# Graph attention on one core: rulers ahead of the gathers, and a new order for the last steps

## The chip, the cores and the metric

The kernel runs on one core of a Trainium2 chip. The metric is the time of one execution on the device in microseconds (us), the median of several runs; lower is better. A core has five engines with a queue of instructions each: TensorE (PE, matrix products and transposes; its weight loads are listed as PEld), VectorE (DVE), ScalarE (ACT), GpSimd (POOL) and SyncE (SP). Transfers are started by an instruction in one of the queues and then run by themselves on 16 DMA engines; in the listings SPq and ACTq are the starts of transfers in the queues of SP and ACT. SBUF is the on-chip memory (128 partitions), PSUM the small memory into which PE writes.

## What is computed

One layer of a graph network: N = 12,500 nodes with 128 features, E = 212,500 edges sorted by their destination, 8 heads of 16 features.

```python
h = relu(layernorm(x))                       # nodes
q = h @ Wq.T + bq;  v = h @ Wv.T + bv        # nodes
k = edge_attr @ Wk.T + bk                    # edges
qs, qd = q[src], q[dst]                      # edges
in_m, out_m, diag_m = sum(qs * k), sum(qd * k), sum(qs * qd)   # over each head's 16
score = (softmax_by_dst(in_m * SCALE) + softmax_by_dst(out_m * SCALE)
         + softmax_by_dst(diag_m * SCALE)) * edge_weight ** lam
agg = segment_sum(score * v[dst], dst)
out = x + leaky_relu(agg @ Wo.T + bo, 0.1)
```

As v[dst] is the same for all edges of a segment, the kernel sums only scores (24 numerators and 24 denominators a node) and multiplies by v once for each node.

## The kernel before

All of it is in the function `ordered_path`. The helper `pin` (L596) ties an instruction to the pinned one before it on the same engine, so each engine executes in the written order; the order of the work is therefore written out by hand. Instructions that aren't pinned are placed where they are written, but only their data bind them.

**Preparation** (L734 to L1014). The nodes come in in groups, DVE takes their statistics (L886 to L909), ACT normalizes (L921), PE transposes (L929, copied at L931) and multiplies with Wq (L937), DVE adds the bias (L940), and the rows of q go to a table in HBM, `q_table`. The first 40 gathers on POOL (L691) fetch raw rows of x instead, since the table isn't ready; from the twelfth on they are paced by DVE's groups of nodes. The function `show` (L750 to L758) makes `shows`, a small matrix of "rulers": POOL counts up two tiles by iota (`of_f` L752, `of_row` L755), and DVE compares the first (L757) and casts the second (L758). `raw_indices` (L763 to L768) makes the indices of the raw gathers.

**The main loop.** The edges are cut into 416 blocks of 512; the last one, with 20 edges, is treated apart. The other 415 are spread over S = 5 streams of G = 83 blocks, so that a turn t takes block t of each stream, and a step g = 5t + s handles one block. In each step:

- POOL gathers q[src] for step g + 20, four indirect transfers of 128 rows (`gather`, L691);
- PE transposes the edge features two steps ahead (`turn`, L1154; ACT copies at L1156), multiplies them with Wk one step ahead (`project`, L1161 and L1163), and spreads q[dst] from a window of the table with one-hot matrices (`spread_q`, L1171; ACT copies `qd` at L1174 and makes the one-hots at L1148 and L1149);
- DVE forms the three products (L1184 and L1185) and, once for two steps, sums them over heads' features into the logits `lT` (L1190).

For each turn, two turns later and spread over its steps: PE transposes the logits (`turn_logits`, `l_ps`, L1211), DVE scans forward for the running maximum of each segment (`scan_on`, L1244 and L1249) and back (`scan_back`, L1262), for which ACT first spreads a mask into PSUM (`spread_far`, `far_ps`, L1255); PE turns the maxima (`turn_max`, `m_ps`, L1332), `powers` subtracts them (DVE, L1340) and exponentiates (ACT, L1341), `weigh_powers` multiplies with the weights (L1352), and `to_rows` sums edges into nodes by a matrix product with the selection `sel` (L1380, copied by ACT at L1385). `select` (SP, L1358) loads where the segments end and `show_ends` makes `sel` from it: per turn two products with the rulers into `d_ps` (L1366), two absolute values (L1369) and one rectifier (L1370) on ACT. `put_rows` (SP, L1396) stores the sums of a turn, one transfer a stream, at row addresses that SP has read into its registers in `fetch` (the register load is at L626). `l_ps`, `far_ps`, `m_ps`, `d_ps`, `w_ps` and the nodes' `node_ps` share one ring of three PSUM buffers (`small`, L1202).

**Finishing nodes.** As turns are stored, pairs of node groups are finished between the steps by the class `Nodes`: `load_x`, `load_sums` (SP at L1061, for nodes at the border of two streams also ACT at L1063), `normalize` (L1070), `turn` (L1080, copied at L1083), `project_v` (product with Wv, L1086 and L1088), `scores` (L1030 to L1036), `weigh` (L1096), `project_o` (product with Wo, L1107), `add_x` (L1112 and L1113) and `store` (L1119, L1121). What is at the border of streams can only be finished at the end: `rest`, five groups with 18 tiles of 128 nodes, begun in the last steps by `begin_rest`; the products with Wv that wait for their scores are made by `hold` into banks of PSUM.

**The tail** (L1555 to L1609) is what follows the last step: the logits and scans of the last turns G−2, G−1 and G (G is the block of 20 edges), their powers and sums, the storing of these sums, then `load_sums` of the five groups, the last ordinary pair, and the groups' scores, weighings and outputs. The scores of all 18 tiles are made by one pass of `scores_of`.

Of the kernel before, what the change touches and what calls it, by code (L numbers as in the profile page):

```python
# [472 lines left out]
def ordered_path(ctx: ExitStack, tc: tile.TileContext, flag, x, src, dst, edge_attr, edge_weight,  # L473
# [144 lines left out]
    def fetch(t):  # L618

        if t >= T:  # L620
            return
        far = load.tile([R, BE + 1], BF, name="far", bufs=4)
        lo = t * BE
        of = bass.AP(far_d.tensor, far_d.offset + lo, [[G * BE, S], [0, H3], [1, BE + 1]])
        pin(nc.sync.dma_start(far, of))
        _, base_v[t] = nc.values_load_multi_w_load_instructions(  # L626
            bases[0:1, t:t + (S - 1) * G + 1:G], engines=[mybir.EngineType.SP], min_val=0, max_val=N - 1,
            skip_runtime_bounds_check_because="the indices of nodes are below N")
        st[t] = dict(far=far)
# [104 lines left out]
    with tc.tile_pool(name="prep", bufs=1) as prep, \  # L734
# [14 lines left out]

        def show():  # L750
            of = prep.tile([K4, JN, S, W], F32, name="of_f", tag="of", bufs=2)
            nc.gpsimd.iota(of, pattern=[[1, JN], [JN, S], [0, W]], base=1, channel_multiplier=-1,  # L752
                           allow_small_or_imprecise_dtypes=True)
            row = prep.tile([1, JN, S, W], F32, name="of_row", tag="of", bufs=2)
            nc.gpsimd.iota(row, pattern=[[0, JN], [0, S], [1, W]], base=1, channel_multiplier=0,  # L755
                           allow_small_or_imprecise_dtypes=True)
            nc.vector.tensor_scalar(shows, of, 0.0, -1.0, op0=ALU.is_equal, op1=ALU.mult)  # L757
            nc.vector.tensor_copy(shows[0:1], row)  # L758
# [279 lines left out]
    class Nodes:  # L1038
# [52 lines left out]
        def project_v(self, to):  # L1091
            self.held = to
# [39 lines left out]
    with tc.tile_pool(name="work", bufs=2) as work, \  # L1132
# [228 lines left out]
        def show_ends(t):  # L1361

            sel = st[t]["sel"] = work.tile([P, JN, S, W], F32, name="sel", bufs=3)
# [24 lines left out]
        def put_rows(t, of=range(S)):  # L1388
            for i, (lo, own) in enumerate(trios):
                for k in own:  # L1390
# [5 lines left out]
                    pin(nc.sync.dma_start(  # L1396
# [84 lines left out]
        products = str(mybir.EngineType.PE)  # L1481
        fetch(1)
# [10 lines left out]
        for g in range(end):  # L1493
# [39 lines left out]
            later(put_rows, t - 2 if s == 4 else t - 3, [(s + 1) % S])  # L1533
            if t == G - 1:
                if 0 < s < 4:
                    select(G - 3 + s)
                elif s == 4:
                    for i in (G - 2, G - 1, G):
                        show_ends(i)
# [6 lines left out]
            begin_rest(g - (end - BEGIN))  # L1546
            if g < S:
# [7 lines left out]
        leaving, last_pair = pairs[G - 3], pairs[G - 1]  # L1555
# [3 lines left out]
        last_pair.scores()  # L1559
        last_pair.turn(small([P, JN, P], "node_ps"))  # L1560
        scan_on(G - 1)
        hold(rest[0], True)
        more_banks()
        last_pair.project_v(banks.pop(0))
        scan_back(G - 2)
        turn_max(G - 2)
        scan_on(G)
        scan_back(G - 1)
        turn_max(G - 1)
        scan_back(G)  # L1570
        turn_max(G)
        for t in (G - 2, G - 1, G):
            powers(t)
        for t in (G - 2, G - 1, G):
            weigh_powers(t)
        last_pair.weigh(last_pair.held)
        for t in (G - 2, G - 1, G):
            to_rows(t)
            put_rows(t)
        for r, of in enumerate(rest):  # L1580
            of.load_sums(ends_ab[:, r * JN:r * JN + of.n], of.more)
        hold(rest[1])
# [3 lines left out]
        banks.append(last_pair.held)  # L1586
        hold(rest[4])
        last_pair.turn(small([P, JN, P], "node_ps"))
        last_pair.project_o(small([P, JN, F], "node_ps"))
        last_pair.add_x(nc.vector)  # L1590
        last_pair.store()
        ab = ends_ab[:, :sum(of.n for of in rest)]
        for r, of in enumerate(rest):
            if of.more is not None:
                some = ends_ab[:, r * JN:r * JN + of.n]
                pin(nc.vector.tensor_add(some, some, of.more))
# [58 lines left out]
```

## Time and profile before

| | |
|---|---|
| time before, median of 3 runs | 2207.11 us (2204.27 to 2220.55) |
| the profiled execution | 2203.87 us, span 2201.3 us |
| granted TensorE clock, mean over the span | 0.796 |
| busy share of the span | DVE 89%, PE 78%, POOL 72%, ACT 64% |
| gathers from the table (L691) | 1620, 0.955 us each |
| DMA | 355.66 MB, mean 162 GB/s |

The span is the part of the execution that the profile covers; the profiled execution took 2.57 us more than its span. Rows of a timeline begin with the start and the length of an instruction (or of several alike that follow each other, with their count behind an x), both in us; in brackets stand the idle time of that engine just before and who ended it. Rows of a windows view begin with a stretch and give the busy time of PE, PEld, DVE, ACT and POOL, the granted clock of PE (1.00 is full speed), the share of the DMA engines' time and GB/s. The page's group rows give the number of instructions, their busy time, the mean in ns, and the idle time before them.

### The profile page before, as it was taken

Reading aid. Unit: us, or ns where it says so; the run is one execution under the profiler, and the core shown is the slowest. Engines: PE = TensorE matmul, PEld = TensorE weight load, DVE = VectorE, ACT = ScalarE, POOL = GpSimd, SP = SyncE. Lnnn points to the kernel's source line nnn. Section 1 sums busy time; section 2 is a strip of 40 time slices with the busy share of each in tenths; the row PEclk is TensorE's granted clock in tenths of the full one; section 3 lists DMA queues with packets and bytes.
Section 4 is the critical chain, followed back from the end, with each engine's and each line's share of the span. In section 5 each row is a group of like instructions: output and inputs, shape, how many; then the busy total and the mean of one; then the engine's idle time right before and its main releaser. Section 6 shows DMA issues by size and latency. Waiting matters only on the chain.

```text
span 2201.3 us, 34508 instructions
## 1 busy us (share of the span) xinstructions
PE 1708.5 (78%) x10337; PEld 1362.8 (62%) x10337; DVE 1958.7 (89%) x2140; ACT 1414.6 (64%) x2639; POOL 1595.4 (72%) x1676
## 2 busy tenths in 40 slices
PE   6767777777778786888788778877877888788875
PEld 4545656566566665666666666666665666666664
DVE  7858999999888999989999999999999998988893
ACT  6846666666666666666666766666666666666671
POOL 5677777777777777777777777777777777777750
PEclk9867888878877878777877887787788777877877
DMA  9585554555554555545555554555556545544531
GB/s 260 170 255 152 168 164 148 175 149 162 173 155 146 157 166 176 160 148 156 175 168 154 183 170 147 158 180 157 156 166 183 150 147 164 162 148 145 161 91 58
DMA packets 306062, 355.66 MB, mean 162 GB/s; under 512 B 118195, under 2 KB 225661, under 8 KB 305557
## 3 DMA queue, kind: packets, MB, share of 16 engines
q1 hardware_dynamic: 237258, 238.26, 35.1%
q0 software_dynamic: 53184, 108.92, 17.1%
q10 hardware_dynamic: 15424, 6.19, 1.1%
q8 instruction: 83, 1.36, 0.3%
q14 instruction: 113, 0.93, 0.1%
HBM read 321.34 MB, written 31.85 MB: 160 GB/s over the span
## 4 chain that ended last, share of the span: by engine, by line
PE 37%; DVE 31%; DMA 11%; issue 9%; ACT 4%; POOL 2%; SPq 1%; ACTq 0%; DVEq 0%; POOLq 0%
PE kq_ps L1163 13%; DMA qq<-q_table,src_i 10%; DVE lT L1190 10%; DVE prod L1185 10%; PE w_ps L1380 6%; DVE prod L1184 5%; PE eT_ps L1154 5%; PE kq_ps L1161 4%; DVE u L1244 3%; PE node_ps L1088 3%; PE kq_ps L1171 3%; POOL qq L691 2%; PE d_ps L1366 2%; PE l_ps L1211 1%; ACT relb L1148 1%
## 5 line engine op out<-in xcount | busy, mean ns | idle before, releaser
L691 POOL DMA_INDIRECT qq<-q_table,src_i x1620 | 1547.1, 955 | 494.1 <-issue 233.9
L1163 PEld LDWEIGHTS kq_ps<-wk,eT 128*128 128x128 f32 x3320 | 522.2, 240 | 377.1 <-issue 159.4
L1190 DVE TENSOR_REDUCE lT<-prod 128x192 f32<-128x3072 f32 (+1 forms) x249 | 702.1, 2819 | 8.6
L1163 PE MATMUL kq_ps<-wk,eT 128*128 128x128 f32 x3320 | 617.5, 343 | 7.5 <-ACT eT L1156 6.5
L1174 ACT COPY qd<-kq_ps 128x512 f32<-128x512 f32 x415 | 242.2, 584 | 417.0 <-PE kq_ps L1171 386.0
L1185 DVE TENSOR_TENSOR prod<-qq,kq_ps 128x1024 f32<-128x1024 f32 x415 | 503.2, 1213 | 5.9 <-issue 3.2
L1161 PE MATMUL kq_ps<-b,ones 3*128 3x512 bf16 x415 | 185.6, 447 | 223.0 <-DVE prod L1185 222.8
L1154 PE MATMUL eT_ps<-ident,ea 128*128 128x128 f32 x1660 | 323.5, 330 | 1.0 <-DVE qq L940 1.0
L1148 ACT ACTIVATE relb<-relb,before 114x512 bf16<-114x512 bf16 x415 | 302.6, 729 | 0.0
L1184 DVE TENSOR_TENSOR prod<-qd,kq_ps 128x512 f32<-128x512 f32 x415 | 279.5, 674 | 12.0 <-ACT qd L1174 6.8
L1149 ACT ACTIVATE oh<-relb 114x512 bf16<-114x512 bf16 x415 | 261.4, 630 | 13.6 <-ACT relb L1148 0.4
L1156 ACT COPY eT<-eT_ps 128x512 f32<-128x512 f32 x415 | 244.0, 588 | 37.7 <-PE eT_ps L1154 37.2
L1154 PEld LDWEIGHTS eT_ps<-ident,ea 128*128 128x128 f32 x1660 | 229.1, 175 | 1.1 <-DVE qq L940 1.1
L1380 PE MATMUL w_ps<-back,sel 128*114 128x144 f32 (+1 forms) x1344 | 213.7, 320 | 19.3 <-DVE back L1352 14.8
L1380 PEld LDWEIGHTS w_ps<-back,sel 128*114 128x114 f32 (+1 forms) x1344 | 205.6, 211 | 26.4 <-ACT h L1070 9.2
L1332 PE MATMUL m_ps<-ident,m 120*128 120x120 f32 x332 | 70.9, 347 | 170.3 <-DVE m L1262 167.8
L1171 PE MATMUL kq_ps<-win,oh 114*128 114x128 bf16 x1660 | 199.9, 255 | 2.6 <-DMA win<-q_table 2.6
L1341 ACT ACTIVATE back<-back 128x480 f32<-128x480 f32 x83 | 50.1, 604 | 201.9 <-DVE back L1340 201.9
L1244 DVE TENSOR_TENSOR_SCAN u<-far,u,l_ps 120x512 f32<-120x512 bf16 x82 | 104.7, 1276 | 78.2 <-PE l_ps L1211 77.0
L1171 PEld LDWEIGHTS <-oh 114*128 114x128 bf16 x1660 | 161.2, 118 | 15.5 <-issue 2.8
L1332 PEld LDWEIGHTS m_ps<-ident,m 120*128 120x128 f32 x332 | 50.7, 215 | 192.8 <-DVE m L1262 188.6
L1262 DVE TENSOR_TENSOR_SCAN m<-far_ps,head,u 120x512 f32<-120x512 f32 x81 | 103.1, 1273 | 0.0
(192 smaller groups left out, 1467.4 us busy)
## 6 DMA issues: line engine op xcount, KB each, us to landing
ea<-in_edge_attr_dram SPq DMA_DIRECT2D x83, 1280.0 KB
relb<-rel_d SPq DMA_DIRECT2D x83, 640.0 KB
qq<-q_table,src_i POOLq DMA_INDIRECT x1620
win<-q_table SPq DMA_DIRECT2D x415, 28.5 KB
far<-far_d SPq DMA_DIRECT2D x84, 120.2 KB
q_table<-more_q SPq DMA_DIRECT2D x40, 192.0 KB
sums<-rows SPq DMA_DIRECT2D x412, 7.1 KB
q_table<-xq SPq DMA_DIRECT2D x24, 256.0 KB
```

Of the source, the lines that this page charges most:

```text
L691: rows = pin(nc.gpsimd.indirect_dma_start(out=qq[:, j, :], out_offset=None, in_=x if g < RAW else q_table, in_offset=bass.IndirectOffsetOn ...
L1148: pin(nc.scalar.activation(d, d, AF.Abs, bias=before[:K3]))
L1149: pin(nc.scalar.activation(oh, d, AF.Relu, bias=1.0, scale=-1.0))
L1154: pin(nc.tensor.transpose(eT_ps[:, j, :], eas[g // S][:, g % S, j * F:(j + 1) * F], ident))
L1156: pin(nc.scalar.copy(eT, eT_ps))
L1161: pin(nc.tensor.matmul(k_ps, ones3, bk3, start=True, stop=False))
L1163: pin(nc.tensor.matmul(k_ps[:, j, :], eTs[g][:, j, :], wk, start=False, stop=(j == JN - 1)))
L1171: pin(nc.tensor.matmul(qd_ps[:, j, :], ohs[g][:, j * P:(j + 1) * P], d["win"][:, s, :], start=(j == 0), stop=(j == JN - 1)))
L1184: pin(nc.vector.tensor_mul(prod[:, :, 2, :], qds[g], kqs[g][:, 0]))
L1185: pin(nc.vector.tensor_mul(prod[:, :, 0:2, :], qqs[g][:, :, None, :].to_broadcast([P, JN, 2, F]), kqs[g].rearrange("p i j f -> p j i f")))
L1190: pin(nc.vector.tensor_reduce(lTs[t][:, :, lo:s + 1, :].rearrange("p j s c -> p j (s c)"), prods[0][:, :, :s + 1 - lo].rearrange("p j s i ...
L1380: pin(nc.tensor.matmul(w_ps[:, i].rearrange("p s c -> p (s c)"), d["sel"][:n, j, lo:lo + 3, :].rearrange("p s w -> p (s w)"), d["back"][:n ...
```

## The change

1. Both rulers are counted up ahead of the first gathers on POOL, `of_row` pinned; DVE's two operations that make `shows` of them are pinned where they stand, behind the second `raw_indices`.
2. The register loads in `fetch` are pinned, and for the turns from G−2 on ACT loads the addresses too.
3. The selections of the last turns are loaded in the last turn but one and at the start of the last, and their `show_ends` are in the steps s = 0, 1 and 2 of the last turn instead of all in its step 4; `sel` has four buffers instead of three.
4. The product with Wv of the first group of `rest` and the turn of the last pair are made in the last two steps, the other products of this kind earlier in the tail.
5. In the tail the powers, weights and sums of G−2 come before those of G−1 and G; the last pair's scores come after the sums are stored. For turns from G−2 on, the rows of streams 1 and 3 are stored by ACT's queue.
6. The scores of `rest` are made in two parts, groups 0 and 1 (8 tiles) and groups 2 to 4 (10 tiles), the second behind the weighing of the first two groups; the last pair's output is added and stored there, too. Two of the additions of x (L1113) are on POOL.

```diff
--- before.py
+++ after.py
@@ -623,9 +623,12 @@
         lo = t * BE
         of = bass.AP(far_d.tensor, far_d.offset + lo, [[G * BE, S], [0, H3], [1, BE + 1]])
         pin(nc.sync.dma_start(far, of))
-        _, base_v[t] = nc.values_load_multi_w_load_instructions(
-            bases[0:1, t:t + (S - 1) * G + 1:G], engines=[mybir.EngineType.SP], min_val=0, max_val=N - 1,
+        at = [mybir.EngineType.SP] + [mybir.EngineType.Activation] * (t >= G - 2)
+        loads, base_v[t] = nc.values_load_multi_w_load_instructions(
+            bases[0:1, t:t + (S - 1) * G + 1:G], engines=at, min_val=0, max_val=N - 1,
             skip_runtime_bounds_check_because="the indices of nodes are below N")
+        for load_of in loads:
+            pin(load_of)
         st[t] = dict(far=far)
 
     def fetch_places(t):
@@ -747,15 +750,16 @@
             if lo == 0:
                 pin(nc.sync.dma_start(bq_all, bq[None, :].to_broadcast([P, F])))
 
+        of_f = prep.tile([K4, JN, S, W], F32, name="of_f", tag="of", bufs=2)
+        nc.gpsimd.iota(of_f, pattern=[[1, JN], [JN, S], [0, W]], base=1, channel_multiplier=-1,
+                       allow_small_or_imprecise_dtypes=True)
+        of_row = prep.tile([1, JN, S, W], F32, name="of_row", tag="of", bufs=2)
+        pin(nc.gpsimd.iota(of_row, pattern=[[0, JN], [0, S], [1, W]], base=1, channel_multiplier=0,
+                           allow_small_or_imprecise_dtypes=True))
+
         def show():
-            of = prep.tile([K4, JN, S, W], F32, name="of_f", tag="of", bufs=2)
-            nc.gpsimd.iota(of, pattern=[[1, JN], [JN, S], [0, W]], base=1, channel_multiplier=-1,
-                           allow_small_or_imprecise_dtypes=True)
-            row = prep.tile([1, JN, S, W], F32, name="of_row", tag="of", bufs=2)
-            nc.gpsimd.iota(row, pattern=[[0, JN], [0, S], [1, W]], base=1, channel_multiplier=0,
-                           allow_small_or_imprecise_dtypes=True)
-            nc.vector.tensor_scalar(shows, of, 0.0, -1.0, op0=ALU.is_equal, op1=ALU.mult)
-            nc.vector.tensor_copy(shows[0:1], row)
+            pin(nc.vector.tensor_scalar(shows, of_f, 0.0, -1.0, op0=ALU.is_equal, op1=ALU.mult))
+            pin(nc.vector.tensor_copy(shows[0:1], of_row))
 
         raw_f = prep.tile([S, LEAD, P, JN], F32, name="raw_f", tag="weight")
 
@@ -1089,7 +1093,7 @@
                                      stop=(b == self.n - 1)))
 
         def project_v(self, to):
-            self.held = to
+            self.held = self.v = to
             self.product(to, bv3, wv)
 
         def weigh(self, to):
@@ -1360,7 +1364,7 @@
 
         def show_ends(t):
 
-            sel = st[t]["sel"] = work.tile([P, JN, S, W], F32, name="sel", bufs=3)
+            sel = st[t]["sel"] = work.tile([P, JN, S, W], F32, name="sel", bufs=4)
             for i in range(0, JN, 2):
                 d = small([P, 2, S, W], "d_ps")
                 pin(nc.tensor.matmul(d.rearrange("p j s w -> p (j s w)"), ends_t[t % 2 if t < G - 1 else t - G + 3],
@@ -1393,7 +1397,7 @@
                         continue
                     first = 1 if t == 0 and s > 0 else 0
                     upto = 1 if t == T - 1 and s < S - 1 else W
-                    pin(nc.sync.dma_start(
+                    pin((nc.scalar if t >= G - 2 and s % 2 else nc.sync).dma_start(
                         sums[s][first:NP][bass.ds(base_v[t][s], upto - first), t % 2, :],
                         st[t]["rows"][k * W + first:k * W + upto, i, k, :]))
             if S - 1 in of:
@@ -1479,6 +1483,7 @@
             banks.extend([both[:, 0], both[:, 1]])
 
         products = str(mybir.EngineType.PE)
+        leaving, last_pair = pairs[G - 3], pairs[G - 1]
         fetch(1)
         fetch_rows(0)
         fetch_places(1)
@@ -1531,12 +1536,16 @@
             if ahead > 1:
                 fetch_rows(ahead, [k])
             later(put_rows, t - 2 if s == 4 else t - 3, [(s + 1) % S])
+            if t == G - 2 and 0 < s < 3:
+                select(G - 2 + s)
             if t == G - 1:
-                if 0 < s < 4:
-                    select(G - 3 + s)
-                elif s == 4:
-                    for i in (G - 2, G - 1, G):
-                        show_ends(i)
+                if s == 0:
+                    select(G - 2)
+                    show_ends(G - 1)
+                elif s == 1:
+                    show_ends(G)
+                elif s == 2:
+                    show_ends(G - 2)
             behind[g + 1, 3] = pinned[products]
             nodes_between(t, s)
             if s < 3:
@@ -1544,6 +1553,11 @@
             if g == 12 * S:
                 examine()
             begin_rest(g - (end - BEGIN))
+            if g == end - 2:
+                hold(rest[0], True)
+            if g == end - 1:
+                last_pair.turn(small([P, JN, P], "node_ps"))
+                more_banks()
             if g < S:
                 of = [u for u in range(NU) if g in parts_of(u)]
                 pin(nc.scalar.dma_start(
@@ -1552,60 +1566,66 @@
                     blank[:, None, :].to_broadcast([P, 2 * len(of), 2 * 2 * H3])))
 
 
-        leaving, last_pair = pairs[G - 3], pairs[G - 1]
         leaving.store()
         put_rows(G - 3, range(1, S))
         turn_logits(G - 1)
-        last_pair.scores()
-        last_pair.turn(small([P, JN, P], "node_ps"))
+        last_pair.project_v(banks.pop(0))
         scan_on(G - 1)
-        hold(rest[0], True)
-        more_banks()
-        last_pair.project_v(banks.pop(0))
         scan_back(G - 2)
+        hold(rest[1])
         turn_max(G - 2)
         scan_on(G)
+        powers(G - 2)
         scan_back(G - 1)
         turn_max(G - 1)
+        weigh_powers(G - 2)
         scan_back(G)
         turn_max(G)
-        for t in (G - 2, G - 1, G):
-            powers(t)
-        for t in (G - 2, G - 1, G):
-            weigh_powers(t)
-        last_pair.weigh(last_pair.held)
-        for t in (G - 2, G - 1, G):
+        to_rows(G - 2)
+        powers(G - 1)
+        powers(G)
+        weigh_powers(G - 1)
+        weigh_powers(G)
+        put_rows(G - 2)
+        for t in (G - 1, G):
             to_rows(t)
             put_rows(t)
+        last_pair.scores()
+        last_pair.weigh(last_pair.held)
         for r, of in enumerate(rest):
             of.load_sums(ends_ab[:, r * JN:r * JN + of.n], of.more)
-        hold(rest[1])
         more_banks()
         for r in (2, 3):
             hold(rest[r])
-        banks.append(last_pair.held)
-        hold(rest[4])
         last_pair.turn(small([P, JN, P], "node_ps"))
         last_pair.project_o(small([P, JN, F], "node_ps"))
-        last_pair.add_x(nc.vector)
-        last_pair.store()
-        ab = ends_ab[:, :sum(of.n for of in rest)]
-        for r, of in enumerate(rest):
-            if of.more is not None:
-                some = ends_ab[:, r * JN:r * JN + of.n]
-                pin(nc.vector.tensor_add(some, some, of.more))
+        banks.append(last_pair.v)
+        hold(rest[4])
         score = scan.tile([P, len(rest) * JN, HEADS], F32, name="end_score", bufs=1)
-        scores_of(ab, score[:, :ab.shape[1]])
-        for r, of in enumerate(rest):
-            of.score = score[:, r * JN:(r + 1) * JN]
+        tiles = [r * JN for r in range(len(rest))] + [sum(of.n for of in rest)]
+
+        def end_scores(lo, hi):
+            for r in range(lo, hi):
+                if rest[r].more is not None:
+                    some = ends_ab[:, tiles[r]:tiles[r + 1]]
+                    pin(nc.vector.tensor_add(some, some, rest[r].more))
+            scores_of(ends_ab[:, tiles[lo]:tiles[hi]], score[:, tiles[lo]:tiles[hi]])
+            for r in range(lo, hi):
+                rest[r].score = score[:, tiles[r]:tiles[r + 1]]
+
+        end_scores(0, 2)
         for r in range(len(rest) + 2):
             if r < len(rest):
                 rest[r].weigh(rest[r].held)
+            if r == 1:
+                last_pair.add_x(nc.gpsimd)
+                last_pair.store()
+                end_scores(2, len(rest))
             if 0 <= r - 1 < len(rest):
                 rest[r - 1].turn(small([P, JN, P], "node_ps"))
             if 0 <= r - 2:
                 rest[r - 2].project_o(small([P, JN, F], "node_ps"))
-                rest[r - 2].add_x(nc.vector)
+                rest[r - 2].add_x(nc.gpsimd if r == 2 else nc.vector)
                 rest[r - 2].store()
```

## The prediction

> **What bounds the kernel now.** I read the page's busy times and groups first, then the windows, then the timelines of the two ends.
>
> ```profile
> PE 1708.5 (78%) x10337; PEld 1362.8 (62%) x10337; DVE 1958.7 (89%) x2140; ACT 1414.6 (64%) x2639; POOL 1595.4 (72%) x1676
> ...
> L691 POOL DMA_INDIRECT qq<-q_table,src_i x1620 | 1547.1, 955 | 494.1 <-issue 233.9
> ```
>
> The busy shares point to VectorE (DVE, 89%), and mislead. The group of L691 holds GpSimd's (POOL's) gathers of table rows: 1547.1 us busy and 494.1 idle over 1620 of them, so 0.955 + 0.305 = 1.26 us each, and together 2041.2 us of the 2201.3. The gap is in front of every gather and mostly "issue", which means that nothing shown is waited for. So from the first table gather to the last, POOL is one unbroken stream, and the length of the middle is 1620 gathers by 1.26 us. The change takes no gather out and makes none shorter. It can only move the start of the stream, and what follows its end:
>
> ```profile
> 2128.12:2201.30 73.18, 45.06 (x223) 35.31 (x220) 36.62 (x53) 18.40 (x36) 2.45 (x5) 0.69 0.16 49
> ```
>
> This windows row (busy time of PE, PE's weight loads, DVE, ACT, POOL; granted clock; DMA share; GB/s) is the 73 us after the last gather was issued. No engine is full there: it is a chain of waits, and its order is what the change rewrites.
>
> **A. The rulers in front of the gathers.** Timeline rows of the head, each with its start, its length and, in brackets, the idle time before it and who ended it:
>
> ```profile
> 12.33 0.29 DVE L886 BATCH_NORM_STATS2 stats<-xq 128x6 f32<-128x128 f32 x1
> ...
> 19.28 0.55 DVE L758 CAST shows<-of_row 1x760 bf16<-1x760 f32 x1 [6.66 <-POOL of_row L755]
> 19.75 2.20 DVE L886 BATCH_NORM_STATS2 stats<-xq 128x6 f32<-128x128 f32 x11
> ...
> 4.49 1.11 POOL L691 DMA_INDIRECT qq<-in_x_dram,raw_i  x1 [1.61 <-DVE raw_i L768]
> ...
> 18.11 1.13 POOL L755 IOTA of_row<- 1x760 f32 x1
> ...
> 80.76 4.69 POOL L691 DMA_INDIRECT qq<-in_x_dram,raw_i  x1 [0.30 <-issue]
> ...
> 22.70 0.30 ACT L907 ACTIVATE inv<-sums,eps 128x12 f32<-128x12 f32 x1 [10.13 <-DVE sums L899]
> ```
>
> DVE stands 6.66 us at L758 because the ruler of_row is made at 18.11, behind eleven gathers. ACT's first rows of the main preparation (L907) wait 10.13 us for DVE's statistics. After the change of_row comes ahead of the first gather, in POOL's 1.61 us of idle time; 1.13 us fit, so the iota costs nothing, and if the cover were gone it would cost its 1.13. The cast of 0.55 us moves ahead of the memsets. The statistics that began at 19.75 then begin at about 12.33 + 0.29 + 0.55 + 0.6 = 13.8 (0.6 for the moved L757 work and gaps, an estimate): **−6.0 us**. Whether what follows keeps pace is bounded by the transfers:
>
> ```profile
> 20.00:40.00 20.00, 14.99 (x87) 12.53 (x87) 16.92 (x81) 16.40 (x42) 6.64 (x7) 1.00 0.95 238
> 19.28:85.76 66.48, 54.25 (x337) 42.05 (x337) 57.85 (x237) 58.85 (x152) 31.16 (x30) 1.00 0.74 217
> ```
>
> The row at 80.76 is the last gather before those of the table, which begin 0.31 behind its end, at 85.76. Between 19.28 and there the DMA engines are busy 0.74 of the time; the same bytes in 60.5 us need a share of 0.81, which fits, and ACT with 58.85 of 66.48 us is what sets the pace. But in 20–40 the share is already 0.95: squeezed to 1.0, that stretch could shrink by 1 us only. So A lies between −6.0 and −1; I take −6.0, since the row for the whole stretch has the room and the statistics wait for a ruler, not for a transfer. What starts earlier at 85.76 is the saturated stream, which carries the gain whole to its end. That includes the register loads and pins in the fetches: the steady order of SP's queue is unchanged.
>
> **B. Selections and show_ends a turn earlier.** Each show_ends takes two PSUM buffers of the ring of three named "small" (d_ps) and about 1.7 us of ACT. Before, three stood in the last product step; now they stand in steps s = 0, 1, 2 of the last turn.
>
> ```profile
> 2116.06 0.60 PE L1080 MATMUL node_ps<-ident,h 128*128 128x128 f32 x4
> 2119.18 0.37 PE L1161 MATMUL kq_ps<-b,ones 3*128 3x512 bf16 x1 [2.53 <-DVE prod L1185]
> ...
> 2121.69 1.06 PE L1154 MATMUL eT_ps<-ident,ea 128*128 128x128 f32 x4
> 2123.76 0.75 PE L1332 MATMUL m_ps<-ident,m 120*128 120x120 f32 x4 [1.02 <-DVE m L1262]
> ...
> 2122.44 1.27 DVE L1262 TENSOR_TENSOR_SCAN m<-far_ps,head,u 120x512 f32<-120x512 f32 x1
> ...
> 2125.34 0.65 DVE L1340 TENSOR_TENSOR back<-lT,m_ps 128x480 f32<-128x480 f32 x1
> ...
> 2128.22 0.87 ACT L1369 ACTIVATE sel<-d_ps 128x380 f32<-128x380 f32 x2
> 2129.12 0.84 ACT L1370 ACTIVATE sel<-sel 128x760 f32<-128x760 f32 x1
> ...
> 2120.00:2140.00 20.00, 15.87 (x71) 11.48 (x70) 18.52 (x21) 10.30 (x22) 8.44 (x12) 0.67 0.18 52
> 2126.40:2136.70 10.30, 9.30 (x38) 7.06 (x38) 10.20 (x10) 5.47 (x13) 3.56 (x7) 0.50 0.07 19
> ```
>
> One far_ps holds a buffer of that ring until DVE's backward scan (L1262) has read it. With the d_ps between them, the node turn (L1080, at 2116.06 now) gets the buffer of far_ps, so it must wait for the scan's end, and PE works in order: behind the turn stand the projection, the spread and the edge transposes of a product step, then the transposes m_ps (L1332) for which DVE's L1340 waits. From the scan's end that is 0.60 (turn) + 3.57 (a step, 2119.18 to 2122.75, at the low clock) + 0.75 = 4.92 us, and now L1340 starts 1.63 us after the scan's end. So a new stall of 3.3 us; with PE's parts halved (full clock) 2.46 − 1.63 = 0.8. I take **+2.5**, nearer to the slow end, as the windows show 0.67 and 0.50 granted here. ACT's 3 × 1.71 us are covered: in 2120–2140 it is busy 10.30 of 20. SP's selects leave earlier, nothing on SP waits behind them.
>
> **C. From the last product to the first load of sums.**
>
> ```profile
> 2133.42 1.75 DVE L1190 TENSOR_REDUCE lT<-prod 128x96 f32<-128x1536 f32 x1
> ...
> 2135.89 1.39 PE L1366 MATMUL d_ps<-shows,ends_t 21*128 21x380 bf16 x3
> ...
> 2139.06 0.65 PE L1211 MATMUL l_ps<-ident,lT 128*120 128x128 f32 x4
> ...
> 2141.89 2.08 PE L1088 MATMUL eT_ps<-wv,qq 128*128 128x128 f32 x8
> ...
> 2148.03 0.60 ACT L1341 ACTIVATE back<-back 128x480 f32<-128x480 f32 x1 [5.98 <-DVE back L1340]
> ...
> 2157.95 0.40 ACT L1385 COPY rows<-w_ps 114x288 f32<-114x288 f32 x1 [1.78 <-PE w_ps L1380]
> ...
> 2137.83 24.60 SPq L1396 DMA_DIRECT2D sums<-rows  x19
> ...
> L626 SPq TENSOR_LOAD <-bases x84: 1271/1578/5297, 115.4 to 2158.9; - x84
> ```
>
> The last products end at 2135.17, but l_ps starts at 2139.06: PE does the d_ps first, 2135.89 to 2139.06, 3.2 us in step with ACT. They leave: −3.2. The product with Wv in eT_ps and the last pair's turn also go ahead of l_ps, but into 2126.4–2136.7, where PE is busy 9.30 of 10.30 us: moved, not hidden, 0. The second such product (L1086 and L1088, 0.5 + 2.08) now stands ahead of m_ps: +2.6. The exponentials of the turns G−1 and G stand on ACT behind rows(G−2): one copy of 0.40, two exponentials of 0.60 and the product with the weights, about 0.65 as L1340: +2.3. At SP's end the register load (the one at 2158.9 is among its shortest, 1.3) leaves the chain, and two of the five last puts go to ACT's queue; puts on SP follow each other by some 0.42 (19 in 24.60 us with waits, so at most 1.3): −1.3 − 0.8 = −2.1. Sum C: −3.2 + 2.6 + 2.3 − 2.1 = **−0.4**. If PE bounds throughout, the exponentials hide and it is −2.7; if the moved d_ps meet a full PE, +2.8.
>
> The new operations on ACT have no row: its register loads (three, in turns G−4 to G−2) are bounded by SP's, 1.27 to 5.30, and taken at the median of 1.58, hidden in ACT's idle 36%; a put on ACT by ACT's own loads below, 4.80/7 = 0.69, behind copies that it needs anyway.
>
> **D. The end scores in two parts.**
>
> ```profile
> 2162.08 4.80 ACTq L1063 DMA_DIRECT2D qq<-sums  x7
> 2162.48 5.60 SPq L1061 DMA_DIRECT2D ends_ab<-sums  x9
> ...
> 2163.79 3.15 DMA qq<-sums
> ...
> 2170.31 0.69 DVE L1112 TENSOR_TENSOR h<-h,node_ps 128x512 f32<-128x512 f32 x1 [14.77 <-ACT h L1107]
> ...
> 2171.64 1.96 DVE L1596 TENSOR_TENSOR ends_ab<-ends_ab,qq 128x384 f32<-128x384 f32 x4
> 2173.63 1.06 DVE L1030 TENSOR_TENSOR ends_ab<-ends_ab 128x864 f32<-128x864 f32 x1
> ...
> 2179.36 0.69 DVE L1096 TENSOR_TENSOR qq<-eT_ps,end_score 128x512 f32<-128x512 f32 x1
> ...
> 2185.30 0.69 DVE L1112 TENSOR_TENSOR qq<-qq,node_ps 128x512 f32<-128x512 f32 x1 [4.06 <-ACT qq L1107]
> ...
> 2136.41 0.35 DVE L1030 TENSOR_TENSOR ab<-ab 128x192 f32<-128x192 f32 x1
> ...
> 2138.35 0.19 DVE L1036 TENSOR_TENSOR score<-score,ab 128x32 f32<-128x32 f32 x1
> ```
>
> From the first load on SP to the first weighing are 2179.36 − 2162.48 = 16.9 us now: DVE stands 14.77 us for the last pair's own chain, then adds four groups, then scores all 18 tiles in 5.73 us (2173.63 to 2179.36). The same six operations over 4 tiles took 2.13 (2136.41 to 2138.54), so a line through both gives 3.2 us for 8 tiles and 3.7 for 10. After: four loads on SP (4 × 0.62), a landing of 3.15, two adds (0.98), 3.2 of scores: 9.8 us, **−7.1**. Behind the first weighing come two adds and the second part, 0.98 + 3.7 = 4.7, the last pair's L1112 (0.69) and a weighing that now stands behind them (0.64); DVE's idle 4.06 takes that much of it: **+1.9**. The bound for D: −4.6 if the first sums land late (rival 3) with the second part unhidden, −8 if all of it is hidden. The two adds moved to POOL are unseen here: by POOL's rows an elementwise operation lies between 1.13 (the iota) and the 4.69 of a gather beside DVE's work; the first outputs aren't what ends last, so 0 either way up to some 4 us.
>
> **Sum.** −6.0 + 2.5 − 0.4 − 7.1 + 1.9 = −9.1 us. The profiled execution took 2203.87 us (span 2201.3 and 2.57 around it), so 2194.8 for a like one; that execution is 3.2 below the median of 2207.11, and against the median it is **2198**. One per cent, 22 us, is about what a measurement of this kernel can tell from no change.
>
> **The rivals.**
> 1. *The head is bound by transfers* (chance 0.15). For it: the share of 0.95 in 20–40. Against: 0.74 over the whole stretch, and the wait of 6.66 names the ruler. A becomes −1 to −3, the total about −5: 2202.
> 2. *PE gets the full clock in the last turns and the tail* (0.08). Then B is 0.8, and the 45.06 us of PE behind the last gather, granted 0.69, shrink to 31.1: 14 us less, of which I count 8, an estimate, as on the chain: −9.1 − 1.7 − 8 = −19, 2188. Against: in 2126.4–2136.7 PE was busy 9.30 of 10.30 us and still had 0.50. The Trainium skill, "TensorE: Matmul & The Clock Gate", Part 1, has the gate open after some 3.4 us of sustained work, by which this rival would be the rule. That row disagrees with it, hence the low chance.
> 3. *The split scores gain little* (0.10): the nine loads land together, first two groups at 2171 as now; D's first term is then 2171.6 + 0.98 + 3.2 − 2179.4 = −3.6: total −5.6, 2201.5.
> 4. *Slower: the register loads on ACT* (0.07). ACT feeds every product (qd, eT and one-hots); a load of SP's longest 5.30 us in each of three turns stops it, three times 5.3 = 15.9 with nothing recovered, since the stream of products is 89% DVE: −9.1 + 15.9 = +6.8, 2214. It decides from 3 us a load on. For it: DVE has little slack. Against: SP's median is 1.58, and the gathers run 20 steps ahead.
>
> The forecast has 0.60, its own range 2193 to 2204 by the bounds of B, C and D (−5 to +6). Rivals 1 and 3 lie inside; the 8 in 10 reach from 2188 (rival 2) to 2209, short of rival 4. No case lies beyond 22 us; by scatter of the runs I leave 0.07 below and 0.05 above.
>
> **What would show each step.** A: L758 with no idle before it, the statistics near 13.8, the first table gather near 79.8 and the last near 2122. B: the turn at L1080 in the last turn waiting for DVE's m, L1340 waiting for PE 1 to 3 us. C: l_ps some 0.5 us behind the last reduction, the last put on SP 1.3 to 2 us sooner after rows. D: two runs of L1030 to L1036, the first weighing 10 us behind the first load, DVE's idle of 4 us gone. The forecast is wrong if the first table gather stays at 85, if ACT's loads cost over 3 us, or if the stream of gathers shows gaps that it hadn't.

## The result and the profile after

The changed kernel took 2198.9 us (median of 19 runs, 2193.37 to 2208.62) against 2209.38 (2201.46 to 2222.61) for the kernel before in as many runs: a ratio of 0.9956 with a 95% interval of 0.9942 to 0.9970, so 10 us less (7 to 13). The prediction said 2198, 9 us less. The size and the side are right. The profile shows that two of the steps behind them were not, and that one sentence about the whole kernel was wrong.

The profiled execution after took 2201.97 us with a span of 2200.1, only 1.2 us less than the span before. It has to be read by stages, not by its end. The head first (timeline rows as before):

```profile
11.09 0.54 DVE L762 CAST shows<-of_row 1x760 bf16<-1x760 f32 x1
...
13.53 2.21 DVE L890 BATCH_NORM_STATS2 stats<-xq 128x6 f32<-128x128 f32 x11
...
2.85 1.49 POOL L757 IOTA of_row<- 1x760 f32 x1
4.97 1.11 POOL L694 DMA_INDIRECT qq<-in_x_dram,raw_i  x1 [0.64 <-DVE raw_i L772]
...
79.39 0.94 POOL L694 DMA_INDIRECT qq<-q_table,src_i  x1 [0.30 <-issue]
```

The cast no longer waits, the statistics begin at 13.53 (13.8 was forecast), and the first gather from the table at 79.39 instead of 85.76: 6.4 us earlier. Now the last gather and the last product, of the kernel before and then of the changed one:

```profile
2128.12 0.94 POOL L691 DMA_INDIRECT qq<-q_table,src_i  x1 [0.30 <-PE d_ps L1366]
...
2132.18 1.21 DVE L1185 TENSOR_TENSOR prod<-qq,kq_ps 128x1024 f32<-128x1024 f32 x1
```

```profile
2118.80 0.94 POOL L694 DMA_INDIRECT qq<-q_table,src_i  x1 [0.30 <-PE node_ps L1084]
...
2141.03 1.21 DVE L1189 TENSOR_TENSOR prod<-qq,kq_ps 128x1024 f32<-128x1024 f32 x1
2142.28 1.75 DVE L1194 TENSOR_REDUCE lT<-prod 128x96 f32<-128x1536 f32 x1
```

The last gather is 9.3 us earlier and the last product 8.9 us later. Before, the product came 4 us behind its gather; after, 22 us. In the profile after, no product waited for a gather, so there the gathers did not set the end of the loop. In the profile before, three products did wait, 5.7 us in all, from 1928 us on. The windows, cut at the same events, show where the time lies: the steps up to the last turn, the last turn, the last reduction to the first load of sums, from there to the first weighing of the rest, and on to the last addition. First the kernel before, then the changed one (the columns as in the prediction):

```profile
120.30:2112.20 1991.90, 1569.61 (x9571) 1254.32 (x9570) 1821.38 (x1740) 1294.81 (x2358) 1508.84 (x1584) 0.79 0.54 163
...
2112.22:2135.17 22.95, 17.27 (x93) 13.88 (x92) 21.03 (x19) 14.11 (x29) 14.39 (x18) 0.74 0.26 72
2135.17:2162.48 27.31, 24.96 (x127) 19.43 (x126) 11.84 (x22) 8.77 (x17) 0.00 (x0) 0.72 0.05 14
2162.48:2179.36 16.88, 3.19 (x17) 2.43 (x15) 8.77 (x13) 1.18 (x2) 0.00 (x0) 0.65 0.37 110
2179.36:2193.99 14.63, 10.79 (x59) 8.28 (x59) 8.99 (x15) 5.28 (x10) 0.00 (x0) 0.83 0.16 53
```

```profile
115.90:2118.50 2002.60, 1577.22 (x9554) 1263.74 (x9553) 1822.03 (x1741) 1292.20 (x2352) 1516.81 (x1595) 0.79 0.54 163
...
2118.46:2144.03 25.57, 19.67 (x128) 14.52 (x128) 21.41 (x19) 22.05 (x46) 2.54 (x6) 0.93 0.10 30
2144.03:2164.51 20.48, 15.89 (x92) 13.31 (x92) 11.67 (x22) 2.74 (x6) 0.00 (x0) 0.82 0.07 19
2164.51:2173.15 8.64, 6.26 (x27) 4.81 (x26) 4.09 (x8) 1.18 (x2) 0.00 (x0) 0.70 0.63 184
2173.15:2192.70 19.55, 13.66 (x59) 10.26 (x59) 14.48 (x23) 5.38 (x10) 2.71 (x2) 0.63 0.17 55
```

| stage | before | after | change | forecast |
|---|---|---|---|---|
| start to the first product | 120.3 | 115.9 | −4.4 | A −6.0 |
| first product to the last turn | 1991.9 | 2002.6 | +10.7 | 0 |
| last turn | 22.95 | 25.57 | +2.6 | B +2.5 |
| last reduction to first load of sums | 27.31 | 20.48 | −6.8 | C −0.4 |
| first load to first weighing | 16.88 | 8.64 | −8.2 | D −7.1 |
| first weighing to last addition | 14.63 | 19.55 | +4.9 | D +1.9 |

Without the second row the stages give −11.9, near the measured −10.5. That second row has to be explained first. DVE's busy time in it is the same in both (1821.4 and 1822.0): what grew is waiting. The waits of DVE between 180 and 2100 us (us in total, times, longest), before and after:

```profile
DVE u L1244 <- PE l_ps L1211: 75.8, 45, 4.2
...
DVE prod L1185 <- DMA qq<-q_table,src_i: 2.5, 1, 2.5
...
DVE prod L1185 <- issue: 1.5, 1, 1.5
```

```profile
DVE u L1248 <- PE l_ps L1215: 86.9, 47, 4.1
```

In more than half of the turns DVE stands until PE has turned the logits (l_ps). That is the largest wait of DVE in the loop, and it grew by 11.1 us. Its size changes with the run. Over 128 runs of before, after and the experiments on ordinary chips, a line with one offset for each kernel and a common slope gives 8.0 us (± 0.8, one standard error) more for each 0.01 less of mean granted clock, with 3.9 us of scatter left. In the ten profiles of these chips, DVE's whole wait in front of this scan is 92 to 98 us at the clocks from 0.783 to 0.788 and 67 to 93 at those from 0.794 to 0.799. The clocks of the two profiles here, 0.796 and 0.795, are too close to explain the 10.7 us. But the profiled run before lies 5.5 us below the median of its kernel and the one after 3.1 above its own, and that is 8.6 of them. What makes a single run longer at the same clock is not shown. So one profile against another says little about the loop; medians and the other stages say more.

### The profile page after: what moved, and what is told of

It reads as the page before. It is cut to its first block, busy times and chain, and to the rows that moved or that the text cites. A ratio compares the mean times of both kernels' runs of the same rounds, so it can differ in the third digit from the quotient of the medians.

```text
span 2200.1 us, 34526 instructions
## 1 busy us (share of the span) xinstructions
PE 1715.9 (78%) x10337; PEld 1370.5 (62%) x10337; DVE 1961.2 (89%) x2144; ACT 1414.0 (64%) x2639; POOL 1595.9 (73%) x1678
## 4 chain that ended last, share of the span: by engine, by line
PE 37%; DVE 28%; DMA 12%; issue 10%; ACT 5%; POOL 3%; SPq 1%; DVEq 0%; ACTq 0%; POOLq 0%
PE kq_ps L1167 13%; DMA qq<-q_table,src_i 12%; DVE prod L1189 9%; DVE lT L1194 8%; PE w_ps L1384 6%; PE eT_ps L1158 5%; DVE prod L1188 5%; PE kq_ps L1165 3%; DVE u L1248 3%; PE kq_ps L1175 3%; POOL qq L694 3%; PE node_ps L1092 3%; PE d_ps L1370 2%; PE l_ps L1215 1%; ACT eT L1160 1%
## 5 line engine op out<-in xcount | busy, mean ns | idle before, releaser
L1384 PE MATMUL w_ps<-back,sel 128*114 128x144 f32 (+1 forms) x1344 | 215.5, 322 | 20.5 <-DVE back L1356 11.7
L1266 DVE TENSOR_TENSOR_SCAN m<-far_ps,head,u 120x512 f32<-120x512 f32 x81 | 103.2, 1274 | 0.0
```

Of the source, the lines that this page charges most:

```text
L1384: pin(nc.tensor.matmul(w_ps[:, i].rearrange("p s c -> p (s c)"), d["sel"][:n, j, lo:lo + 3, :].rearrange("p s w -> p (s w)"), d["back"][:n ...
```

## The experiments

The first four ran on another chip, on which the kernel before itself took 2662 us; there the products end 95 to 102 us behind the gathers. Their ratios can't be set beside those of the other runs; the stages of their tails can, with care. The same kernel (part 3 undone) took 28.4 us from the last reduction to the first load there and 24.7 on an ordinary chip.

**The rulers alone** (the kernel before with part 1):

```diff
+        of_f = prep.tile(...); nc.gpsimd.iota(of_f, ...)
+        of_row = prep.tile(...); pin(nc.gpsimd.iota(of_row, ...))
         def show():
-            nc.gpsimd.iota(of, ...); nc.gpsimd.iota(row, ...)
...
+            pin(nc.vector.tensor_scalar(shows, of_f, ...)); pin(nc.vector.tensor_copy(shows[0:1], of_row))
```

> The kernel before with part 1 alone (both rulers ahead of the gathers). By the prediction, step A, the saturated gathers carry 6.0 us to the end: -6 against before. Rival: the last products are not at the heels of the gathers, the end of the loop is set by VectorE's and TensorE's own pace; then only the earlier start of the products counts (121.0 to 116.5 in the two profiles): -4.5, or less where the pace differs. If the head were bound by transfers: -1 to -3.

Measured there: ratio 0.9996 (0.9978 to 1.0015), no gain that could be told. The gathers from the table do begin earlier there (83.8 us, and 88.5 in the next run, which lacks the rulers), but the first product hardly does: 153.6 against 154.8, and 153.5 and 159.2 in the other two profiles of that chip, which have the rulers. Again on an ordinary chip:

> The same kernel as x1_rulers (the kernel before with part 1 alone). By now the theory is that the products, not the gathers, set the end of the loop, and that what the products gain at their start is carried: the first product 4.4 us earlier (120.3 to 115.9): -4.4 against before. By the prediction's step A: -6. Rival: the loop gives it back, 0.

Measured: 2202.21 against 2209.04, ratio 0.9962 (0.9947 to 0.9978): 8.4 us less (5 to 12). The first product starts at 115.83, as in the changed kernel:

```profile
115.83 0.69 DVE L1185 TENSOR_TENSOR prod<-qd,kq_ps 128x512 f32<-128x512 f32 x1 [2.12 <-ACT qd L1175]
```

Part 1 brings its gain to the end, 4.4 by the start of the products, and it alone comes near to the gain of the whole change. Why the median shows some 4 us more than the products' start is not settled; with 9 runs and their scatter it may be no more than that. Another candidate is that earlier gathers spare the products their waits: in this profile, too, no product waited for a gather, and in the one before three did (5.7 us). No run separates the two.

**The change without the rulers**:

```diff
-        of_row = ...; pin(nc.gpsimd.iota(of_row, ...))   # part 1 undone
```

> The changed kernel with part 1 undone: the last steps alone. By the prediction's sum B + C + D: +2.5 - 0.4 - 7.1 + 1.9 = -3.1 against before. By the profile after, from the last reduction to the end 10.1 us less (66.1 to 56.1), less the new stall of 3 in the last turn: -7. If the parts add, x1 and x2 together give the change's -10.5.

Measured there: 0.9987 (0.9974 to 1.0001), 3.5 us less. The last steps alone gain little even where their tail is 7 us shorter (last reduction to the end 56.5 us, with the rulers alone 63.4): their last turn is 5 us longer (26.1 us, with the rulers alone 21.1).

**Which stream sets the end of the loop.** Two delays in the changed kernel, one for each stream:

```diff
+                if g == RAW:
+                    for _ in range(30):
+                        pin(nc.gpsimd.memset(pad, 0.0))
```

> The changed kernel with 30 extra memsets of 128x384 on POOL (about 12 us) ahead of the first gather from the table: the stream of gathers starts later, nothing else is touched. If the gathers set the end of the loop, as the prediction has it: +12 against the changed kernel. If VectorE and TensorE set it, 20 us behind the gathers as in the profile after: 0 to +3.

```diff
             logits(g)
+            if g == 100:
+                for _ in range(26):
+                    pin(nc.vector.memset(pad, 0.0))
```

> The changed kernel with 26 extra memsets of 128x384 on VectorE (about 10 us by its 0.4 a piece) in step 100. If the gathers set the end of the loop: 0 to +3 against the changed kernel, since VectorE has the 300 steps behind to make it up. If VectorE and TensorE set it: +10.

Timeline rows of the first with its products' waits for gathers between 180 and 2100 us, and the row of the memsets' line of the second:

```profile
79.05 14.21 POOL L693 MEMSET pad<- 128x384 f32 x30
93.90 0.95 POOL L698 DMA_INDIRECT qq<-q_table,src_i  x1 [0.64 <-DMA q_table<-q]
...
2130.93 0.94 POOL L698 DMA_INDIRECT qq<-q_table,src_i  x1 [0.30 <-issue]
...
2139.01 1.21 DVE L1193 TENSOR_TENSOR prod<-qq,kq_ps 128x1024 f32<-128x1024 f32 x1
...
DVE prod L1193 <- DMA qq<-q_table,src_i: 8.9, 4, 3.6
DVE prod L1193 <- issue: 4.2, 2, 2.2
```

```profile
L1516 DVE MEMSET pad<- x26: 378/378/378, 587.2 to 600.4; 128x384 f32 x26
```

The gathers start 14.5 us later. The ratio is 0.9972 (0.9952 to 0.9992), 0.0016 over the changed kernel's 0.9956: 3.5 us of 14.2. The 26 memsets of 0.378 us on DVE, 9.8 us in all, give 0.9999 (0.9979 to 1.0018), 9.5 us over the changed kernel. Both ran on one chip, where their medians are 2202.30 and 2210.30: the smaller delay cost more. With 300 steps behind it, DVE makes up nothing that could be seen: the products set the end. The gathers are a floor under it, and a run whose products reach their heels waits there. The profile with the late gathers, the fastest of its 12 runs, shows this: its products waited seven times from 1931 us on, 15.3 us in all with one wait behind 2100 us. In the profile with the late products, none waited for a gather, and so it is in seven of the ten profiles on ordinary chips.

**Part 3 undone** (selections and show_ends where they were):

```diff
-            if t == G - 2 and 0 < s < 3: select(G - 2 + s)
             if t == G - 1:
-                if s == 0: select(G - 2); show_ends(G - 1)
-                elif s == 1: show_ends(G)
-                elif s == 2: show_ends(G - 2)
+                if 0 < s < 4: select(G - 3 + s)
+                elif s == 4:
+                    for i in (G - 2, G - 1, G): show_ends(i)
```

> The changed kernel with the selections and show_ends of the last turns where they were before (part 3 undone). By the prediction the stall of 2.5 us in the last turn goes and the 3.2 us of d_ps ahead of l_ps come back: +0.7 against the changed kernel. If the stall costs nothing, because the products are late anyway or the wait only moves: +3.2. If the ring of PSUM buffers costs more than seen: below 0.

Measured there: 0.9996 (0.9979 to 1.0013), with 64.4 us from the last reduction to the end. On an ordinary chip:

> The same kernel as x3_show_late (part 3 undone). From the last reduction to the end it took 64.4 us where the changed kernel takes 56.1; the last turn has a stall of some 2.6 us less. So the theory now: +8.4 - 2.6 = +6 against the changed kernel, or about -4.5 against before. By the prediction: +0.7 against the changed kernel, -10 against before.

Measured: 2190.56 against 2209.04, ratio 0.9920 (0.9904 to 0.9937): the fastest of all versions, and its interval lies wholly below that of the changed kernel. The expectation was on the wrong side. Its profile:

```profile
2142.16 1.75 DVE L1194 TENSOR_REDUCE lT<-prod 128x96 f32<-128x1536 f32 x1
...
2146.98 1.11 PE L1215 MATMUL l_ps<-ident,lT 128*120 128x128 f32 x4 [0.59 <-ACT sel L1373]
...
2168.59 3.14 SPq L1065 DMA_DIRECT2D ends_ab<-sums  x6
```

The last turn is 21.98 us long here (25.57 in the changed kernel: the stall is gone), and from the last reduction to the first load are 24.7 us (20.5): −3.6 and +4.2. So part 3 gains about as much behind the loop as it loses in the last turn. The 7 runs say more than that, some 8 us in its favour, but the profiled one (2206.25 us) was the slowest of the seven, the others lie at 2189.6 to 2197.3. Its mean clock was 0.783, theirs 0.793 to 0.800; by the line above that is 8 to 14 us. At equal clock the same line leaves 4.7 us (± 1.8) in favour of this version. Where these come from, and whether its clock is higher by more than chance, isn't shown.

**Another place for show_ends**, with POOL's additions on DVE:

```diff
             if t == G - 1:
-                if s == 0: select(G - 2); show_ends(G - 1)
-                elif s == 1: show_ends(G)
-                elif s == 2: show_ends(G - 2)
+                if s == 0: select(G - 2)
+                elif s == 2: show_ends(G); show_ends(G - 2)
+            if t == G - 2 and s == 4: show_ends(G - 1)
```

> A version that may beat both: the changed kernel with show_ends of G-1 in the last step of turn G-2 and those of G and G-2 in step 2 of the last turn, so that none stands between far_ps and the node turn, and the two additions on VectorE. If the ring of PSUM buffers makes the stall of 2.6 us in the last turn, it goes: -2 to -3 against the changed kernel, -13 against before. Rival: the d_ps only make another instruction wait, or VectorE's pace is what it is: 0.

Measured: 0.9948 (0.9931 to 0.9966), the same as the changed kernel. The last turn fell to 24.39 us, and l_ps then came 3.5 us behind the last reduction instead of 0.15. The d_ps only made other work wait.

**Part 4 undone** (product with Wv and turn in the tail):

```diff
-            if g == end - 2: hold(rest[0], True)
-            if g == end - 1: last_pair.turn(...); more_banks()
...
         turn_logits(G - 1)
+        last_pair.turn(small([P, JN, P], "node_ps"))
         scan_on(G - 1)
+        hold(rest[0], True); more_banks(); last_pair.project_v(banks.pop(0))
```

> The changed kernel with the first product with Wv for the rest, and the last pair's turn, made in the tail again (part 4 undone). The prediction put the move at 0 (moved, not hidden). Theory now: in the profile after these products run at 2136.9 to 2138.4 while VectorE reduces, and the way from l_ps to m_ps fell from 7.2 to 4.2 us because of it: +3 to +4 from the last reduction to the first load, and in the time.

Measured: 0.9947 (0.9926 to 0.9968), no loss. The last reduction to the first load took 21.9 us against 20.5: 1.4, not 3 to 4.

**One part of scores:**

```diff
-        end_scores(0, 2)
+        end_scores(0, len(rest))
...
-                end_scores(2, len(rest))
```

> The changed kernel with the end scores of all 18 tiles in one pass again; the last pair's scores and output stay where the change put them. By the prediction's step D the split is worth 7.1 - 1.9 = 5.2 us: +5 against the changed kernel. Rival: what step D gained comes from the last pair's chain being off VectorE's path, and the split itself gives little, as its second part (4.7 us) is paid behind the first weighing: between -1 and +1.

Measured there: 0.9987 (0.9973 to 1.0002), like the change without rulers. DVE's rows around the first weighing, and SP's first load:

```profile
2628.47 0.56 DVE L1611 TENSOR_TENSOR ends_ab<-ends_ab,qq 128x384 f32<-128x384 f32 x1 [0.85 <-DMA ends_ab<-sums]
...
2634.79 0.69 DVE L1100 TENSOR_TENSOR qq<-eT_ps,end_score 128x512 f32<-128x512 f32 x1
...
2620.88 6.24 SPq L1065 DMA_DIRECT2D ends_ab<-sums  x9
```

First load to first weighing: 13.91 us (8.64 split); from there to the last addition 14.73 (19.55 split). +5.3 and −4.8: the split brings nothing that lasts. The two other profiles of that chip with split scores say the same: 8.75 and 8.91, then 19.28 and 19.27. What is left of step D, 16.88 to 13.91, goes with the last pair's chain being off DVE's way.

**One queue for the rows, no register loads on ACT:**

```diff
-        at = [SP] + [Activation] * (t >= G - 2)
+        at = [SP]
-                    pin((nc.scalar if t >= G - 2 and s % 2 else nc.sync).dma_start(
+                    pin(nc.sync.dma_start(
```

> The changed kernel with all rows stored by SP's queue and no register loads on ACT. By the prediction's step C two puts of 0.42 return to the end of SP's chain: +0.8 against the changed kernel. Rival: ACT's loads and puts cost more than they save: below 0.

Measured: 0.9953 (0.9926 to 0.9980), no difference; the last reduction to the first load took 20.26 us (20.48 with two queues). Its end alone, from the last copy of rows to the first load, took 1.99 us, with two queues 1.26: the split brings 0.7 us there, too little to show in the time. This profiled execution (2187.82 us) is the fastest of all that were profiled, and its products waited 11.4 us for gathers: with the rulers, too, a run can reach the floor.

**The additions on DVE:**

```diff
-                last_pair.add_x(nc.gpsimd)
+                last_pair.add_x(nc.vector)
-                rest[r - 2].add_x(nc.gpsimd if r == 2 else nc.vector)
+                rest[r - 2].add_x(nc.vector)
```

> The changed kernel with the two additions of POOL back on VectorE. By the prediction 0 (the outputs concerned aren't the last). By the profile after, VectorE would do 1.4 us more behind the first weighing, of which its idle 3.2 us can take the one behind the second part: 0 to +0.7.

Measured: 0.9939 (0.9902 to 0.9976), not to be told from 0.9956. The rows show that POOL's help is none, first the changed kernel, then this one:

```profile
2174.95 2.09 DVE L1611 TENSOR_TENSOR ends_ab<-ends_ab,qq 128x384 f32<-128x384 f32 x2
...
2175.18 1.45 POOL L1117 TENSOR_TENSOR x_in<-h,x_in 128x512 f32<-128x512 f32 x1 [50.30 <-DVE h L1116]
```

```profile
2174.08 0.69 DVE L1117 TENSOR_TENSOR x_in<-h,x_in 128x512 f32<-128x512 f32 x1
2174.69 1.02 DVE L1611 TENSOR_TENSOR ends_ab<-ends_ab,qq 128x384 f32<-128x384 f32 x2
```

POOL takes 1.45 us for the addition, and DVE's two additions at the same time take 2.09 instead of 1.02. DVE is spared 0.69 and pays 1.07.

## Why the prediction held, and where it did not

**The bound.** "One unbroken stream" was a true reading of POOL and the wrong conclusion. A stream without gaps sets the end only if the others wait for it. In the profile before they did so in the last tenth of the loop (three waits, 5.7 us), where the products had come up to the gathers; it was one of that kernel's faster runs (2203.87, median 2209.38). The delays of both streams showed that the products carry a delay in full and the gathers a quarter of it (each size known to some 5 us). So the sentence holds for a run whose products catch up with the gathers, like the one that it was read from, and not for the others.

**A.** The ruler was the cause of the wait, the statistics began within 0.3 us of the forecast, and the gain reached the end, but mostly by another carrier. Where no product waits for a gather, what counts is the first product, 4.4 us earlier, not the first gather, 6.4 us earlier. Rival 1 (transfers bind the head) is refuted by 79.39.

**B.** +2.6 as forecast (+2.5), and through the ring; against the last turn of the rulers alone (21.9 us), in which no product waits for a gather, it is +3.7. But the releaser was another:

```profile
2125.27 0.66 PE L1084 MATMUL node_ps<-ident,qq 128*128 128x128 f32 x4 [2.63 <-ACT sel L1373]
...
2133.18 0.66 DVE L1344 TENSOR_TENSOR back<-lT,m_ps 128x480 f32<-128x480 f32 x1 [2.10 <-PE m_ps L1336]
```

The turn waited 2.63 us for ACT to read d_ps, and went on before the scan of L1266 began at 2127.70. ACT, called covered, is busy 22.05 of 25.57 us in the last turn.

**C.** −0.4 forecast, −6.8 found. The stage has four parts, one for each term:

| part | forecast | before | after | change |
|---|---|---|---|---|
| last reduction to l_ps | −3.2 | 3.89 | 0.15 | −3.7 |
| l_ps to m_ps | +2.6 | 7.24 | 4.16 | −3.1 |
| m_ps to the end of the last copy of rows | +2.3 | 12.05 | 14.91 | +2.9 |
| from there to the first load | −2.1 | 4.13 | 1.26 | −2.9 |

Three terms came within 0.8 us. The term that was mis-sized is the second. The "+2.6" for a second product with Wv ahead of m_ps counted a product that only takes the place of another one there: PE did two between l_ps and m_ps before, and two after, and the turn (1.12 us) in addition before. The rest is PE's pace: such a product took 2.08 us before, as the prediction's row at 2141.89 shows, and 1.16 after. The rows that divide the parts, where the prediction doesn't show them, are one of before and then those of after, that product among them:

```profile
2146.30 1.81 PE L1332 MATMUL m_ps<-ident,m 120*128 120x120 f32 x8
```

```profile
2144.18 0.62 PE L1215 MATMUL l_ps<-ident,lT 128*120 128x128 f32 x4 [0.89 <-DVE lT L1194]
...
2145.05 1.16 PE L1092 MATMUL kq_ps<-wv,hT 128*128 128x128 f32 x8
...
2148.34 0.71 PE L1336 MATMUL m_ps<-ident,m 120*128 120x120 f32 x4 [0.72 <-DVE m L1266]
...
2162.85 0.40 ACT L1389 COPY rows<-w_ps 114x288 f32<-114x288 f32 x1 [1.74 <-PE w_ps L1384]
```

Not all of the −6.8 comes from the change, because the tail in the profile before was a slow one. The rulers alone, with the same code in the tail, took 24.0 us for this stage. The 48 products that sum the rows show the difference, first before, at a granted clock of 0.75, then in the rulers alone, at 1.00:

```profile
2149.51 8.36 PE L1380 MATMUL w_ps<-back,sel 128*114 128x144 f32 x48 [0.60 <-DVE back L1352]
...
2153.27 6.29 PE L1381 MATMUL w_ps<-back,sel 128*114 128x144 f32 x48 [1.27 <-DVE back L1353]
```

Against that profile C is −3.5, and the last turn with C and both parts of D comes to −3.5 as well (+3.7, −3.5, −8.2 and +4.5), less than what the rulers bring. Rival 4 is refuted by the row of ACT's three register loads (shortest, median, longest in ns):

```profile
L627 ACTq TENSOR_LOAD <-bases x3: 1102/1110/1117, 2066.3 to 2114.5; - x3
```

Rival 2 came in part: the clock was 0.93 in the last turn and 0.82 behind it (0.74 and 0.72 before), but 0.63 at the end (0.83).

**D.** −8.2 and +4.9 for −7.1 and +1.9, net −3.3 for −5.2. The second part was priced by DVE alone; behind the first weighing PE has the clock at 0.63 (0.83 before), and DVE still waits there:

```profile
2185.84 0.69 DVE L1116 TENSOR_TENSOR qq<-qq,node_ps 128x512 f32<-128x512 f32 x1 [3.18 <-ACT qq L1111]
```

The idle time that was to hide the second part shrank from 4.06 to 3.18 us only. Rival 3's outcome is what happened in effect: the split gains nothing, though its first sums did land early. The bounds that the prediction gives for D, −4.6 and −8, don't follow from its rows either: its own terms give +2.4 (−3.6 and an unhidden 6.0) and −7.1.

So the total came out by errors of opposite sign, which is luck: A too large by 1.6 and D by 1.9, C too small by 6.4. And the rulers alone give a gain that can't be told from the whole change's.

## What to carry to other kernels

An engine without gaps is not yet the bound: set the n-th item of the stream beside the n-th use of it, at several places, and see who trails whom by how much; a small delay put into each stream settles it in two runs. Where the two streams are as close as here, one run can be bound by the first and the next by the second, and a single profile shows only one of the two. When work is moved ahead of a wait, count what stood there before as well as what stands there now. Splitting a step so that its first half ends earlier gains only if its second half falls into idle time that is really there afterwards.

## What the runs showed of the hardware

- An addition on POOL (1.45 us) doubled two additions on DVE that ran beside it: 2.09 us against 1.02.
- The time followed PE's mean granted clock, 8 us for 0.01 over 128 runs, in a kernel whose busiest engine is DVE. That this goes through DVE's waits for PE is argued from ten profiles; no run isolates it.
- The same 48 matmuls of the same tail took 8.36 us at a granted clock of 0.75 and 6.29 at 1.00, in two profiles.
- On one chip the same kernel took 2662 us instead of 2207 to 2209, with the same mean time of a gather on POOL (0.953 us there) but waits between engines that named no releaser.
